# Two conditioned convolution layers on one core: order of the weight blocks, full-width weight products, and the small network in shifted steps

## The chip, the cores and the metric

The program runs on one core of one Trainium2 chip. The metric is the device time of one execution in microseconds (us), and the median of several runs is compared. The profile is of one execution of its own, so times read from its trace are those of that execution.

## The reference

Two layers are applied in turn to an activation `x` of 32 x 32 samples, 64 channels and 256 positions. In each layer the weights of a 3-tap convolution are made by a small network, for each of 32 x 256 places of its own. Cut to what matters:

```
def conv_ref(x, z, W1, b1, g1, be1, W2, b2, Wb1, bb1, gb1, beb1, Wb2, bb2):
    h = relu(ln(z @ W1 + b1, g1, be1))                 # z: (32, 256, 16) -> h: (32, 256, 128)
    w = (h @ W2 + b2).reshape(B, L, CI, CO, K)         # 128 -> 64 * 64 * 3 weights for each place
    hb = relu(ln(z @ Wb1 + bb1, gb1, beb1))
    bias = (hb @ Wb2 + bb2).transpose(0, 2, 1)         # (32, 64, 256)
    x_uf = stack([pad(x)[..., i:i + L] for i in range(K)], axis=-1)
    return einsum('sbilk,bliok->sbol', x_uf, w) + bias[None]

x = x + conv_ref(group_norm(x), ...layer 0...)
x = x + conv_ref(group_norm(x), ...layer 1...)
```

All is float32. The group norm has 32 groups over the last axis and takes its statistics over the whole of a sample's values in a group.

## The kernel before

**Rounds.** The work of a layer is cut into 32 units `u` (4 samples of the batch, 64 of the 256 positions each), and a unit into two halves `h` of the output channels. The main loop runs over `v`, 128 rounds for both layers. In round `v` the weights of half `v` are made (`weights`, 12 blocks) and the products of half `v - 1` are taken (`products`). The order within a round is written out by hand: `weights(v, 0)` makes its first block, then come the products of the round before (`between`), then the eviction of that block and the other 11 blocks, with the side work of `agenda(v)` behind them.

**Blocks.** A block is one tile `pg` (128 x 8 x 128, three buffers in PSUM) with the weights of 8 output channels of one *kind*. The convolution pairs even and odd positions, so a tile holds two of the three taps: the lower 64 partitions one tap, the upper 64 another. `make` takes two products for each of the 8 channels: 64 columns of `w2` against one half of the hidden tile `h` (its even or its odd positions). Kinds 0 and 1 use the same half of `h` for both, kind 2 uses even below and odd above. `take` adds the bias `b2` and writes into the one tile `wall`: kinds 0 and 1 with one VectorE addition over 128 partitions, kind 2 (its two halves go to different places) with a VectorE addition of the lower half and eight ScalarE activations of the upper. Each round goes through four groups of 8 channels, kinds 0, 1, 2 in each. `products` reads all of `wall` and `xn`, in 32-column products, and VectorE adds the result to `ring`, which holds residual and bias.

**The opening.** Before the rounds, `first_phase` walks through 22 steps `i`. Each takes statistics of four pieces of `x` on VectorE (`stats`) and reloads the piece's buffer, one of four. Among the steps stand the small network (`Batch`, 8 batches of four hidden tiles), and from step 6 on the 12 blocks of round 0 (`first_weights`). A batch has links in this order: `form` (TensorE), `variance` (VectorE, ScalarE), `scale` (VectorE, GpSimd), `turn` (TensorE transposes, a copy on ScalarE), `hidden` (TensorE, ScalarE, stores to `hd` in DRAM) and four times `bias` (TensorE, ScalarE, stores to `bd` in DRAM). Batch j begins in step 1 + 2j with form, variance and scale, turns in the next, has its hidden tiles in the one after and its four biases in the fourth. Step 18 (`needed`) has the statistics that the first norm needs; steps 18 and 19 merge them, lay the table and normalize the first tile (`starting`).

**Queues.** All loads go through SP's queue in program order, so a load that waits for its buffer holds those behind it. The stores of hidden tiles and biases are issued by ScalarE, between its own operations.

Of the kernel before, what the change touches and what calls it, by code (L numbers as in the profile page):

```python
# [23 lines left out]
FP = mybir.dt.float32  # L24
# [19 lines left out]
def conv_layers(  # L44
# [40 lines left out]
    hd = [dram.tile([P, 2 * 2 * M], FP, name=f"hd_{i}") for i in range(U // 2)]  # L85
    bd = [dram.tile([2, NT, C, LT], FP, name=f"bd_{i}") for i in range(U // 2)]
# [51 lines left out]
    def load_hidden(i):  # L138

        h = hp.tile([P, 2, 2, M], FP, tag="hT", name="hT")  # L140
        nc.sync.dma_start(out=h.rearrange("p b a m -> p (b a m)"), in_=hd[i])
        for b in range(2):
            hs[2 * i + b] = h[:, b]
# [78 lines left out]
    class Batch:  # L222


        def __init__(self, nets, zts, zps, zs, j):
            self.j, self.zt, self.zp, self.zs = j, zts[j % 2], zps[j % 2], zs
# [8 lines left out]

            self.q = take(BLK)
            self.zq = take(2 * BLK).rearrange("p (n f) -> p n f", n=2)
            self.ht = [[take(2 * BLK) for _ in range(2)] for _ in range(2)]
            self.bs = [take(BLK // 2).rearrange("p (t a m) -> p t a m", t=NT, a=2) for _ in range(2)]
            self.var = take(2 * NR * NR)  # L240
# [49 lines left out]
        def hidden(self, net):  # L290
# [8 lines left out]
            for k in range(2):  # L299
# [9 lines left out]
                for r in range(2):  # L309
                    nc.scalar.dma_start(  # L310
                        out=hd[self.j * NR + 2 * k + r], in_=self.ht[0][k][:, r * BLK : (r + 1) * BLK]
                    )

        def bias(self, i):
# [12 lines left out]
            bs = self.bs[i % 2]  # L327
# [115 lines left out]
    def first_phase(first_weights, first_bias, add_bias, starting):  # L443
# [22 lines left out]
        with tc.tile_pool(name="stage", bufs=1) as stage:  # L466
            zts, zps = [], []
            for j in range(2):
                zts.append(stage.tile([P, BLK], FP, name=f"zt_{j}"))
                zps.append(stage.tile([P, NR * NR * A], FP, name=f"zp_{j}"))  # L470
                nc.gpsimd.memset(zts[j], 1.0)
            zs = raw[:, 0 : 2 * BLK].rearrange("p (n r a) -> p n r a", n=2, a=R)

            def load_z(j):
                if j < U // 2 // NR:
                    n, i = divmod(j * NR, UL // 2)
                    for r in range(NR):
                        nc.sync.dma_start(
                            out=zts[j % 2][r * R : r * R + A],
                            in_=layers[n]["z"][:, (i + r) * BLK : (i + r + 1) * BLK],  # L480
                        )
                    w = NR * NR * A
                    nc.sync.dma_start(out=zps[j % 2], in_=layers[n]["zp"][:, i // NR * w : (i // NR + 1) * w])
# [5 lines left out]
            nets.append(Network(stage, layers[1], 1))  # L489
            nc.gpsimd.memset(zs, 0.0)  # L490
            load(2)
            load(3)
            load_z(1)
            for n in range(NL):
                load_b2(n)
            stats(0, range(LAND))
            nets[0].prepare(stage)
            count = U // 2 // NR
            made = {}
            begins = {1 + 2 * j: j for j in range(count)}  # L500

            def begun(i):
                j = begins.get(i)
                return None if j is None else made[j]

            for i in range(1, units):
                b = begun(i - 3)
                if b:
                    for k in range(NR):
                        b.bias(k)  # L510
                b = begun(i - 2)
                if b:
                    b.hidden(0)
                    b.hidden(1)
                b = begun(i - 1)
                if b:
                    b.turn()
# [416 lines left out]
```

## Time and profile before

| | |
|---|---|
| median of 3 runs | 4251.6 us (4250.24 to 4263.0) |
| profiled execution: its time | 4265.69 us |
| profiled execution: its span | 4263.9 us |
| TensorE products, weight loads, busy | 90%, 86% of the span |
| VectorE, ScalarE, GpSimd, busy | 61%, 30%, 45% |
| granted TensorE clock, mean | 0.986 |
| HBM read and written | 496.91 MB, 148.90 MB |

The page puts the time of an execution into its engines. A record of a float32 product is one of its two passes, records overlap, and a weight load runs beside the products. So a pace is read from the starts of records, and a wait from the time between the start of one and that of the next.

### The profile page before, as it was taken

How to read it: one execution, taken by the hardware profiler on the slowest of the kernel's cores; microseconds unless marked ns; L12 is line 12 of the kernel's file. 1: busy time of each engine (PE TensorE's matmuls, PEld its weight loads, DVE VectorE, ACT ScalarE, POOL GpSimd, SP SyncE). 2: the span in 40 equal slices, each digit the busy share in tenths (PEclk: the TensorE clock that was granted, in tenths of full speed). 3: DMA queues.
4: the chain of work that ended last, by engine and by line, in shares of the span. 5: the costliest groups of instructions: out<-in, count | busy, mean ns of one | idle time of the engine just before them, and what ended most of it. 6: DMA issues, size and time to landing. Idle time of an engine off the chain costs nothing.

```text
span 4263.9 us, 185545 instructions
## 1 busy us (share of the span) xinstructions
PE 3827.1 (90%) x86548; PEld 3683.7 (86%) x86548; DVE 2586.3 (61%) x2954; ACT 1288.1 (30%) x4431; POOL 1935.4 (45%) x655
## 2 busy tenths in 40 slices
PE   5669999999999999999998999999999999999998
PEld 3368898989989889899988999989889898898988
DVE  3366776777767776666665555555555555555555
ACT  2323233332333323323233222322323222232222
POOL 1034444444453444444454555545445544544551
PEclk9779999999999999999999999999999999999999
DMA  6565564655546555444478676777867777777772
GB/s 214 166 219 160 180 180 154 191 167 181 178 155 187 170 165 156 125 151 140 136 175 159 143 143 132 150 130 148 140 136 147 130 155 132 132 147 132 155 130 81
DMA packets 648724, 657.77 MB, mean 154 GB/s; under 512 B 563848, under 2 KB 572432, under 8 KB 582160
## 3 DMA queue, kind: packets, MB, share of 16 engines
q1 hardware_dynamic: 625936, 633.31, 61.7%
q8 instruction: 677, 11.09, 1.2%
q10 hardware_dynamic: 22016, 12.59, 1.0%
q14 instruction: 95, 0.78, 0.1%
HBM read 496.91 MB, written 148.90 MB: 151 GB/s over the span
## 4 chain that ended last, share of the span: by engine, by line
PE 74%; DMA 4%; ACT 4%; issue 4%; DVE 3%; POOL 2%; SPq 1%; ACTq 0%; POOLq 0%
PE pg L634 45%; PE pc L688 22%; PE pg L635 7%; DMA bt<-bd 4%; ACT wall L657 4%; DVE wall L646 3%; POOL ring L578 2%; SPq L571 1%; SPq L184 0%; DVE ring L697 0%; PE spread L419 0%; SPq L728 0%; SPq L583 0%; PE pe L598 0%; DVE first_parts L735 0%
## 5 line engine op out<-in xcount | busy, mean ns | idle before, releaser
L634 PE MATMUL pg<-hT,w2t 128*64 128x128 f32 x24576 | 2750.5, 274 | 28.9 <-issue 19.3
L635 PE MATMUL pg<-hT,w2t 128*64 128x128 f32 x24576 | 2752.7, 274 | 18.0 <-issue 17.6
L634 PEld LDWEIGHTS pg<-hT,w2t 128*64 128x64 f32 x24576 | 2687.2, 137 | 61.4 <-issue 39.3
L635 PEld LDWEIGHTS pg<-hT,w2t 128*64 128x64 f32 x24576 | 2686.9, 137 | 25.4 <-issue 24.8
L646 DVE TENSOR_TENSOR wall<-pg,b 128x1024 f32<-128x1024 f32 (+1 forms) x1536 | 1871.9, 1219 | 687.0 <-PE pg L635 681.2
L657 ACT ACTIVATE wall<-pg,b 64x128 f32<-64x128 f32 x4096 | 1158.2, 462 | 2191.5 <-DVE wall L646 2187.6
L688 PE MATMUL pc<-wall,xn 128*32 128x128 f32 (+1 forms) x36864 | 953.2, 263 | 282.1 <-ACT wall L657 137.4
L688 PEld LDWEIGHTS pc<-wall,xn 128*32 128x32 f32 x36864 | 917.9, 111 | 327.3 <-ACT wall L657 154.6
L578 POOL TENSOR_TENSOR ring<-ring,bt 128x2048 f32<-128x2048 f32 x127 | 577.6, 4548 | 1309.5 <-DMA bt<-bd 1030.8
L697 DVE TENSOR_TENSOR ring<-pc,ring 128x512 f32<-128x512 f32 x512 | 353.9, 691 | 843.3 <-PE pc L688 843.3
L620 POOL TENSOR_TENSOR xn<-raw,tab 128x2112 f32<-128x2112 f32 x86 | 438.9, 5104 | 568.0 <-PE pc L688 521.7
L620 POOL TENSOR_TENSOR xn<-xn,tab 128x2112 f32<-128x2112 f32 x126 | 591.8, 4697 | 9.9
L620 POOL TENSOR_TENSOR xn<-land,tab 128x2112 f32<-128x2112 f32 x40 | 224.7, 5617 | 106.4 <-DMA land<-x 106.2
L344 DVE BATCH_NORM_STATS2 parts<-ring 128x6 f32<-128x256 f32 x512 | 192.1, 417 | 6.5
L593 ACT COPY rim<-ring 128x64 f32<-128x64 f32 x64 | 19.5, 305 | 532.6 <-DVE ring L697 516.2
L735 DVE BATCH_NORM_STATS2 first_parts<-land 128x6 f32<-128x512 f32 x168 | 114.2, 680 | 3.0 <-DMA land<-in_xg_dram 2.9
L274 POOL TENSOR_TENSOR raw<-zp,xn 128x256 f32<-128x256 f32 x16 | 10.3, 644 | 173.5 <-DVE xn L269 82.9
L298 PE MATMUL ph<-xn,wc 17*128 17x512 f32 x128 | 41.3, 1061 | 39.1 <-ACT xn L288 37.7
L436 POOL COPY tab<-spot 64x1024 f32<-64x1024 f32 x28 | 29.0, 1035 | 86.7 <-ACT spot L423 85.8
L298 PEld LDWEIGHTS ph<-xn,wc 17*128 17x128 f32 x128 | 12.6, 295 | 58.2 <-ACT xn L288 39.7
L259 DVE TENSOR_TENSOR xn<-pt,zp 128x256 f32<-128x256 f32 x16 | 6.0, 419 | 74.6 <-PE pt L246 74.6
L461 DVE BATCH_NORM_STATS2 first_parts<-ring 128x6 f32<-128x512 f32 x72 | 44.5, 676 | 10.0 <-DMA ring<-in_xg_dram 9.9
(87 smaller groups left out, 390.2 us busy)
## 6 DMA issues: line engine op xcount, KB each, us to landing
bt<-bd SPq DMA_DIRECT2D x508, 256.0 KB, 10.8
ring<-in_xs_dram SPq DMA_DIRECT2D x64, 1024.0 KB, 11.7
x<-ring SPq DMA_DIRECT2D x64, 1024.0 KB, 4.9
ring<-x SPq DMA_DIRECT2D x64, 1024.0 KB, 9.6
out_dram<-ring SPq DMA_DIRECT2D x64, 1024.0 KB, 4.8
raw<-in_xp_dram SPq DMA_DIRECT2D x55, 1056.0 KB, 14.2
land<-in_xg_dram SPq DMA_DIRECT2D x46, 1024.0 KB, 7.8
raw<-x SPq DMA_DIRECT2D x128, 256.0 KB, 8.9
```

The lines of the kernel that those rows point to most:

```text
L298: nc.tensor.matmul(p[:, r], self.w.wc[x, net], self.zq[x, net], start=True, stop=True)
L344: nc.vector.bn_stats(out, y.rearrange("p o (a m) -> p o a m", a=2)[:, :, :, g * e : (g + 1) * e])
L461: nc.vector.bn_stats(first_parts[:, g, bg], slots[order[i]][:, k])
L578: nc.gpsimd.tensor_tensor(y, y, bts.pop(v), ALU.add)
L620: eng.tensor_tensor(o, i, tab[:, x, None, j0:j1].to_broadcast(list(o.shape)), op)
L634: nc.tensor.matmul(pg[0:C, k, :], w[:, k0 * C : (k0 + 1) * C], h0, start=True, stop=True)
L635: nc.tensor.matmul(pg[C:P, k, :], w[:, k1 * C : (k1 + 1) * C], h1, start=True, stop=True)
L646: nc.vector.tensor_tensor(place(rows, a), pg[rows].rearrange("p o (t m) -> p t m o", t=NT), b2[n][rows, kind, None, None, o0 : o0 + OG].to ...
L657: nc.scalar.activation(place(rows, a)[:, :, :, k], pg[rows, k].rearrange("p (t m) -> p t m", t=NT), AF.Identity, bias=b2[n][rows, kind, o0 ...
L688: nc.tensor.matmul(pc[t * S : (t + 1) * S, n0 - q * EB : n1 - q * EB, :], xn[:, u % 2, t, p, :], wall[:, t, a : a + (n1 - n0) * CH], start ...
L697: nc.vector.tensor_tensor(part, pc.rearrange("p (m a) o -> p o a m", a=2), part, ALU.add)
L735: nc.vector.bn_stats(first_parts[:, g, bg], lands[i % LAND])
```

## The change

Three things change.

1. *Order of the kinds.* A group's blocks are made in the order 0, 2, 1, so that a round ends with kind 1.
2. *Width of the product.* For kinds 0 and 1 one product with 128 columns of `w2` takes the place of two with 64. The 128 columns lie side by side: taps 1 and 2 for kind 0, taps 0 and 1 for kind 1. Kind 2 stays as it was.
3. *The small network.* All of a layer's `z` and `zp` is loaded at once, into the second half of `w2`, which is empty until step 17. All batches exist from the start. Batch j has `form` in step 2j, `variance` and `scale` in step 2j + 1, `turn` in step 2j + 2, `hidden` in step 2j + 3, and two biases each in steps 2j + 4 and 2j + 5. The biases have four buffers in place of two, and hidden tiles and biases are stored by one DMA each in place of two, for which `hd` and `bd` are laid out anew. The batch's buffers lie otherwise in `xn`; the first half of `w2` is loaded ahead of the steps instead of in step 2, the first hidden tiles in step 6 instead of 5, the first bias in step 18 instead of 16, and the blocks of round 0 stand in steps 7 to 18 instead of 6 to 17.

```diff
-    hd = [dram.tile([P, 2 * 2 * M], FP, name=f"hd_{i}") for i in range(U // 2)]
-    bd = [dram.tile([2, NT, C, LT], FP, name=f"bd_{i}") for i in range(U // 2)]
+    hd = [dram.tile([P, 2 * BLK], FP, name=f"hd_{i}") for i in range(U // 4)]
+    bd = [dram.tile([NT, 2, C, LT], FP, name=f"bd_{i}") for i in range(U // 2)]
...
-            self.q = take(BLK)
-            self.zq = take(2 * BLK).rearrange("p (n f) -> p n f", n=2)
-            self.ht = [[take(2 * BLK) for _ in range(2)] for _ in range(2)]
-            self.bs = [take(BLK // 2).rearrange(...) for _ in range(2)]
-            self.var = take(2 * NR * NR)
+            ht = [take(2 * BLK) for _ in range(2)]
+            self.bs = [take(BLK // 2).rearrange(...) for _ in range(4)]
+            self.var = take(2 * NR * NR)
+            o = flat.shape[1] // 2
+            self.ht = [[take(2 * BLK) for _ in range(2)], ht]
+            self.q = take(BLK)
+            self.zq = take(2 * BLK).rearrange("p (n f) -> p n f", n=2)
...
-                for r in range(2):
-                    nc.scalar.dma_start(
-                        out=hd[self.j * NR + 2 * k + r], in_=self.ht[0][k][:, r * BLK : (r + 1) * BLK]
-                    )
+                nc.scalar.dma_start(out=hd[self.j * NR // 2 + k], in_=self.ht[0][k])
...
-            for b in range(2):
-                nc.scalar.dma_start(
-                    out=bd[i][b].rearrange("t o l -> o t l"),
-                    in_=bs[b * C : (b + 1) * C].rearrange("p t a m -> p t (a m)"),
-                )
+            nc.scalar.dma_start(
+                out=bd[i].rearrange("t b o l -> (b o) t l"), in_=bs.rearrange("p t a m -> p t (a m)")
+            )
...
+            half_w2 = w2[:, CH:].rearrange("p o c -> p (o c)")
+            zts = half_w2[:, 0:w].rearrange("p (j f) -> p j f", j=count)
+            zps = half_w2[:, w : w + count * NR * NR * A].rearrange("p (j f) -> p j f", j=count)
+            def load_z(n):
+                js = slice(n * nl, (n + 1) * nl)
+                nc.gpsimd.memset(zts[:, js], 1.0)
+                z = layers[n]["z"].rearrange("a (j r f) -> r a j f", j=nl, r=NR)
+                for r in range(NR):
+                    nc.sync.dma_start(out=zts[r * R : r * R + A, js], in_=z[r])
+                nc.sync.dma_start(out=zps[:, js], in_=layers[n]["zp"].rearrange("p (j f) -> p j f", j=nl))
...
+            load_w2(0, 0, CH)
+            made = [Batch(nets, zts[:, j], zps[:, j], zs, j) for j in range(count)]
+            for i in range(units):
+                j, odd = divmod(i, 2)
+                if batch(j - 2):
+                    for k in range(2 * odd, 2 * odd + 2):
+                        batch(j - 2).bias(k)
+                if odd:
+                    if batch(j):
+                        batch(j).variance()
+                    if batch(j - 1):
+                        batch(j - 1).hidden(0)
+                        batch(j - 1).hidden(1)
+                else:
+                    if batch(j):
+                        batch(j).form()
+                    if batch(j - 1):
+                        batch(j - 1).turn()
...
+                if odd and batch(j):
+                    batch(j).scale()
...
+                if i == needed:
+                    first_bias()
...
-            (k0, h0), (k1, h1) = (((1, odd), (2, odd)), ((0, even), (1, even)), ((2, even), (0, odd)))[kind]
             for k in range(OG):
                 w = w2[:, o0 + k, :]
-                nc.tensor.matmul(pg[0:C, k, :], w[:, k0 * C : (k0 + 1) * C], h0, start=True, stop=True)
-                nc.tensor.matmul(pg[C:P, k, :], w[:, k1 * C : (k1 + 1) * C], h1, start=True, stop=True)
+                if kind < 2:
+                    cols = slice((1 - kind) * C, (3 - kind) * C)
+                    nc.tensor.matmul(pg[:, k, :], w[:, cols], (odd, even)[kind], start=True, stop=True)
+                else:
+                    nc.tensor.matmul(pg[0:C, k, :], w[:, 2 * C :], even, start=True, stop=True)
+                    nc.tensor.matmul(pg[C:P, k, :], w[:, 0:C], odd, start=True, stop=True)
...
-        order = [(kind, o) for o in starts for kind in (0, 1, 2)]
+        order = [(kind, o) for o in starts for kind in (0, 2, 1)]
...
-            if kind == 2 and u % UL == UL - 1 and n + 1 < NL:
+            if kind == 1 and u % UL == UL - 1 and n + 1 < NL:
                 load_w2(n + 1, o0, o0 + OG)
```

## Rows read from the trace of the kernel before

**Rows 1.** The page's costliest groups: busy us, mean ns, idle before and its releasers.

```profile
L634 PE MATMUL pg<-hT,w2t 128*64 128x128 f32 x24576 | 2750.5, 274 | 28.9 <-issue 19.3
L635 PE MATMUL pg<-hT,w2t 128*64 128x128 f32 x24576 | 2752.7, 274 | 18.0 <-issue 17.6
```

**Rows 2.** Timeline of TensorE, first passes of two rounds: start us, us, engine, line.

```profile
2033.35 0.32 PE L634 MATMUL pg<-hT,w2t 128*64 128x128 f32 x1
...
2063.58 0.32 PE L634 MATMUL pg<-hT,w2t 128*64 128x128 f32 x1
```

**Rows 3.** Timelines of VectorE, ScalarE and TensorE at the end of that round.

```profile
2051.08 1.23 DVE L646 TENSOR_TENSOR wall<-pg,b 128x1024 f32<-128x1024 f32 x1 [0.52 <-PE pg L635]
2052.83 1.22 DVE L646 TENSOR_TENSOR wall<-pg,b 64x1024 f32<-64x1024 f32 x1 [0.52 <-PE pg L635]
...
2054.14 2.25 ACT L657 ACTIVATE wall<-pg,b 64x128 f32<-64x128 f32 x8 [2.96 <-DVE wall L646]
...
2054.25 0.27 PE L634 MATMUL pg<-hT,w2t 128*64 128x128 f32 x1
...
2056.44 0.43 PE L688 MATMUL pc<-wall,xn 128*32 128x64 f32 x12 [1.91 <-ACT wall L657]
```

**Rows 4.** Waits of TensorE from 300 us on: us in total, times, longest.

```profile
PE pc L688 <- ACT wall L657: 135.6, 70, 3.7
PE pc L688 <- issue: 117.3, 86, 2.8
```

**Rows 5.** Timelines of VectorE, GpSimd and TensorE over the opening.

```profile
22.61 0.75 DVE L259 TENSOR_TENSOR xn<-pt,zp 128x256 f32<-128x256 f32 x2 [0.97 <-PE pt L246]
...
191.83 0.75 DVE L259 TENSOR_TENSOR xn<-pt,zp 128x256 f32<-128x256 f32 x2 [14.49 <-PE pt L246]
...
214.28 4.52 POOL L578 TENSOR_TENSOR ring<-ring,xn 128x2048 f32<-128x2048 f32 x1 [17.50 <-DMA xn<-bd]
...
250.04 0.43 PE L688 MATMUL pc<-wall,xn 128*32 128x64 f32 x4 [2.80 <-DVE xn L623]
```

**Rows 6.** Windows: us, busy us of PE, PEld, DVE, ACT, POOL (records), granted clock, DMA share, GB/s.

```profile
0.00:250.00 250.00, 137.72 (x824) 84.79 (x824) 89.56 (x175) 83.07 (x146) 27.18 (x48) 0.81 0.61 198
100.00:200.00 100.00, 67.71 (x470) 42.78 (x472) 38.47 (x65) 39.88 (x70) 6.14 (x17) 0.73 0.54 167
```

**Rows 7.** 128-column operations: timeline, one line's records with ns min/median/max, a window's clock.

```profile
1609.16 0.53 PEld L374 LDWEIGHTS over<-apart,same 128*128 128x128 f32 x4
...
L374 PEld LDWEIGHTS over<-apart,same x4: 192/192/193, 1609.2 to 1609.5; 128*128 128x128 f32 x4
...
92.96 2.18 PE L246 MATMUL pt<-form,zt 128*128 128x136 f32 x8 [1.03 <-ACT xn L300]
...
92.90:95.00 2.10, 2.04 (x8) 1.86 (x8) 0.00 (x0) 1.20 (x3) 0.00 (x0) 0.50 0.65 242
```

**Rows 8.** Timelines of TensorE's products and loads around one edge transpose (line 598).

```profile
2005.70 0.27 PE L634 MATMUL pg<-hT,w2t 128*64 128x128 f32 x1
...
2005.90 0.14 PEld L598 LDWEIGHTS pe<-ident,rim 128*128 128x128 f32 x1 [0.17 <-issue]
...
2006.17 0.32 PE L634 MATMUL pg<-hT,w2t 128*64 128x128 f32 x1
...
2006.33 0.27 PE L634 MATMUL pg<-hT,w2t 128*64 128x128 f32 x1
```

**Rows 9.** ScalarE in one batch of the opening (timeline), and its waits up to 250 us.

```profile
149.99 1.37 ACTq L335 DMA_DIRECT2D bd<-xn  x2
154.75 0.47 ACT L328 ACTIVATE xn<-pb,vec 128x256 f32<-128x256 f32 x1 [4.79 <-DMA bd<-xn]
...
160.00 1.20 ACT L300 ACTIVATE xn<-ph,vec 128x1024 f32<-128x1024 f32 x1 [2.18 <-PE ph L298]
161.23 0.82 ACTq L310 DMA_DIRECT2D hd<-xn  x2
...
ACT xn L328 <- DMA bd<-xn: 44.2, 10, 7.6
```

More of the change, by code (lines that the diff above doesn't have):

```diff
@@ L140, in load_hidden @@
         h = hp.tile([P, 2, 2, M], FP, tag="hT", name="hT")
-        nc.sync.dma_start(out=h.rearrange("p b a m -> p (b a m)"), in_=hd[i])
+        nc.sync.dma_start(out=h.rearrange("p b a m -> p (b a m)"), in_=hd[i // 2][:, i % 2 * BLK : (i % 2 + 1) * BLK])
         for b in range(2):
@@ L234, in take @@
                 return flat[:, o - n : o]
+            ht = [take(2 * BLK) for _ in range(2)]
+            self.bs = [take(BLK // 2).rearrange("p (t a m) -> p t a m", t=NT, a=2) for _ in range(4)]
+            self.var = take(2 * NR * NR)
+            o = flat.shape[1] // 2
+            self.ht = [[take(2 * BLK) for _ in range(2)], ht]
             self.q = take(BLK)
             self.zq = take(2 * BLK).rearrange("p (n f) -> p n f", n=2)
-            self.ht = [[take(2 * BLK) for _ in range(2)] for _ in range(2)]
-            self.bs = [take(BLK // 2).rearrange("p (t a m) -> p t a m", t=NT, a=2) for _ in range(2)]
-            self.var = take(2 * NR * NR)
         def form(self):
@@ L466, in first_phase @@
         with tc.tile_pool(name="stage", bufs=1) as stage:
[L467 to L483, printed above, removed]
+            count = U // 2 // NR
+            half_w2 = w2[:, CH:].rearrange("p o c -> p (o c)")
+            w = count * BLK
+            zts = half_w2[:, 0:w].rearrange("p (j f) -> p j f", j=count)
+            zps = half_w2[:, w : w + count * NR * NR * A].rearrange("p (j f) -> p j f", j=count)
+            nl = count // NL
+            def load_z(n):
[4 more added lines that the diff above has]
+                    nc.sync.dma_start(out=zts[r * R : r * R + A, js], in_=z[r])
+                nc.sync.dma_start(
+                    out=zps[:, js], in_=layers[n]["zp"].rearrange("p (j f) -> p j f", j=nl)
+                )
             nets = [Network(stage, layers[0], 0)]
@@ L495, in first_phase, with batch @@
                 load_b2(n)
-            stats(0, range(LAND))
             nets[0].prepare(stage)
[L498 to L517, printed above, removed]
-                if i in begins:
-                    made[begins[i]] = Batch(nets, zts, zps, zs, begins[i])
-                b = begun(i)
-                if b:
-                    b.form()
+            load_w2(0, 0, CH)
+            made = [Batch(nets, zts[:, j], zps[:, j], zs, j) for j in range(count)]
+            def batch(j):
+                return made[j] if 0 <= j < count else None
+            for i in range(units):
[14 more added lines that the diff above has]
+                        batch(j - 1).turn()
                 if i == needed:
@@ L533, in first_phase @@
                 stats(i, range(2))
-                if b:
-                    b.variance()
                 if i == needed:
@@ L538, in first_phase @@
                 stats(i, range(2, LAND))
-                if b:
-                    b.scale()
-                    load_z(b.j + 2)
-                if i == 2:
-                    load_w2(0, 0, CH)
+                if odd and batch(j):
+                    batch(j).scale()
                 if i == 3:
                     nets[1].prepare(stage)
-                if i == 5:
-                    for j in range(2):
-                        load_hidden(j)
-                if i == needed - 3:
+                if i == 6:
+                    for x in range(2):
+                        load_hidden(x)
+                if i == needed - 2:
                     load_half(0, 1, land)
-                if i == needed - 2:
                     load_residual(0)
-                    first_bias()
                 if i == needed - 1:
```

16 lines of the change are left out of this document (9 added, 7 removed).

## The prediction

> **What bounds the kernel now.** I read the page's costliest groups first. The weights products lead: 24576 records on line 634 and as many on 635, each line busy for some 2750 us of the span of 4263.9 [rows 1]. A product leaves two records on its line, one per pass of its float32 operands (128 rounds x 12 blocks x 8 products x 2 = 24576), and the two lines run side by side in the two halves of the array. So their means of 274 ns cannot be added up; the pace is read from a timeline.
>
> The timelines of one clean round (a value of v) give the sum of a round. Its first weights pass starts at 2033.35 and the next round's at 2063.58, so a round lasts 30.23 us [rows 2]. VectorE takes one finished block of weights every 1.75 us (2051.08 to 2052.83) [rows 3]; a block is 8 weights of 2 passes, 16 passes, so a pass (both halves together) costs 0.109 us. The round's last pass on line 634 starts at 2054.25, which is 20.90 us after the first. Then TensorE stands until 2056.44, 2.19 us, and the products run to the next round, 7.14 us [rows 2, 3]. 20.90 + 2.19 + 7.14 = 30.23.
>
> The wait of 2.19 us is the one that can be won. The reader is to see its chain: the last block is of the shared kind, VectorE adds its lower half at 2052.83 for 1.22 us, ScalarE adds the upper half only after that (2054.14, 2.25 us), and the products start 0.05 us later [rows 3]. Over the rounds the list of waits has 135.6 us of products behind that ScalarE line and 117.3 us named "issue" [rows 4]; the two sum to 252.9 us, which is 127 rounds at 1.99 us, so I read most of that "issue" as the same wait under another name. True fetch stalls show where no semaphore is in play: 19.3 + 17.6 = 36.9 us on lines 634 and 635 [rows 1].
>
> Then the opening. Its products start at 250.04 us [rows 5], and 127 rounds of 31.6 us on the mean follow ((4263.9 - 250) / 127). In those 250 us TensorE is busy 137.7 us at a mean granted clock of 0.81, and the DMA engines 61% [rows 6]: nothing is full, so the order of the work sets the pace. VectorE's first small-network product (line 259) comes at 22.61 and its eighth and last at 191.83: 7 batches in 169.2 us, 24.2 us each [rows 5].
>
> **The change part by part.** Times are against the profiled execution's 4265.7 us (span 4263.9); the median of the three runs is 4251.6, 14.1 us lower, and the forecast is given on that scale by taking the same difference off it.
>
> *Shared kind second.* Blocks come as 0, 2, 1, so the round ends on a kind that VectorE alone takes. ScalarE's part now belongs to the last block but one. From that block's last pass to the products takes 3.94 us by ScalarE's chain (2056.44 less 2052.50, which is 16 passes before 2054.25) [rows 3]. In that time TensorE has two blocks of 16 passes left, 32 x 0.111 = 3.55 us, and two mode switches of about 0.19 and 0.20 us (below): 3.94 us. The two chains meet, so the wait falls from 2.19 us to the switch's 0.20 us: **-1.99 us a round**. If ScalarE came 0.5 us later, 0.5 us of it would come back; the three tiles of `pg` do not bind, since the next user of the shared tile comes three blocks later, over 5 us.
>
> *One 128-column product.* For 8 of 12 blocks two half-width products become one full-width product. TensorE's streaming is not cut: two halves already run in one pass of 0.109 us, and the full-width pass streams the same 128 columns of activations. What is new is a weight load of 128 columns per pass instead of two parallel ones of 64. No row shows this very stream at the full clock, so I bound it. Below: a load that hides costs nothing, 0.109 us as now. Above: four 128-column float32 loads with tiny moving operands take 0.53 us, (0.53 - 0.19) / 3 = 0.113 us apart [rows 7], and if the load sets the pace a pass costs that. I take the middle, 0.111: 128 passes a round x 0.002 = **+0.26 us** (0 to +0.51).
>
> *The mode switches.* A round had two changes of column width (64 to 32 and back). With 128, 64, 128 in each of four triples it has seven more: four from 64 to 128, three from 128 to 64. The trace has the pair around the edge transpose, a lone 128-column operation between 64-column passes: pass at 2005.70, its load only at 2005.90, next 64-column pass at 2006.17, and the one after at 2006.33 [rows 8]. In the flow a pass follows after 0.109 us, so 0.09 us is idle before the load. The first load after a switch isn't hidden: the pass after 2006.17 comes 0.16 us later, 0.05 too late for 64 columns; I take 0.10 for 128. Into the wide mode: 0.09 + 0.10 = 0.19; out of it: 0.09 + 0.05, some 0.15. 4 x 0.19 + 3 x 0.15 = **+1.21 us a round** (0.9 if the wide load hides behind the idle time, 1.5 if each switch costs 0.2).
>
> The trace thus shows 0.09 us of standing per switch that no semaphore explains [rows 8]. The Trainium skill, "TensorEngine Tiling (Array Packing)", section Key Properties, says the same as a rule: a change of tiling mode, unlike a change of tile, drains TensorE. By that rule the seven switches each stand 0.09 us and the sum of this part is as above; were it not to hold between 64 and 128 in the steady flow, 7 x 0.09 = 0.63 us a round, 80 us in all, would stay away. The trace agrees with the rule.
>
> Sum of a round: -1.99 + 0.26 + 1.21 = -0.52 us; x 127 = **-66 us** (ends: -1.99 + 0 + 0.9 = -1.09, -138 us; -1.99 + 0.51 + 1.5 = +0.02, +3 us).
>
> *Fewer instructions.* A round's weights go from 768 TensorE instructions to 512. The fetch stalls among them, 36.9 us, fall by up to all of it; I take the same third: **-12 us** (0 to -37).
>
> *The opening.* ScalarE's rows of one batch show why a batch takes 24 us: bias evictions that each wait behind two DMA issues (1.37 us), 4.79 us of waiting for a bias buffer to be written out, and 2.18 us of waiting for the hidden product that needs the turned tile just copied [rows 9]. Over the opening the wait for the biases' writes is 44.2 us in 10 [rows 9]. The change gives the biases four buffers and one DMA issue in place of two, one issue in place of two for the hidden tiles, and sets the links of a batch in different steps (form, then variance, turn, hidden, two and two biases), so that neither wait stands in ScalarE's line. It also loads z once per layer into the unused half of `w2`, so that SP's queue no longer holds a ring load behind a z tile that is in use. What is left for ScalarE in a batch is 9.7 us of work (39.88 in 100 us [rows 6], x 24.2) and its issues, now 4 x 1.37 for biases and 2 x 0.82 for hidden tiles [rows 9], 7.1 us: 16.8, or 13.3 with the issues halved. TensorE has 67.71 us of work in 100 us, 16 us a batch, at a granted clock of 0.73 [rows 6]. So I take 18 us a batch: 7 x 6.2 = 43 us, and some 7 us for the last biases, whose wait stands ahead of the merge: **-50 us**. Ends: 0 if clock or DMA keep the pace, and -75 if the batches come at 15 us (7 x 9.2 = 64, and 11 at the end). The floor is 0.61 x 250 = 152 us of DMA work.
>
> Moved steps: w2's first half (3 MB) now stands on SP's queue ahead of the fifth ring load, and the first bias load comes two steps later, behind w2's second half. Before, the first bias add on GpSimd began at 214.28 after waiting 17.5 us for that load and ended 31 us ahead of the products [rows 5]; two steps of 9 to 12 us use most of that. If it is late, the products' first eviction on VectorE waits, and TensorE behind it: up to 5 us, once. The z fills on GpSimd and the moved 128-column products' VectorE adds change nothing in a round: VectorE has 0.5 us of idle time before each block [rows 3].
>
> Sum: -66 - 12 - 50 = -128 us; 4265.7 - 128 = 4137.7, and on the median's scale 4123.6, so **4124 us**.
>
> **The rivals.**
> 1. *The opening keeps its pace.* DMA at 61% and a clock of 0.73 speak for it, the waits inside ScalarE's line against it. Only the rounds change: -78 us, 4174.
> 2. *Switches or loads cheaper than I take them.* The round gains 1.09 us (-138) and the opening 50 or more, -188 or beyond: 4060. For it speaks that the load of 64 columns hides wholly in the flow, against it the 0.113 us between bare loads.
> 3. *The full-width pass is dearer; slower than before.* One mechanism: each pass of the 8 wide blocks waits for its load. The rest of the change is worth 128 us, 1.0 us a round, 8 ns a pass, so it decides at 0.119 us a pass; at 0.125 the loss is 0.014 x 128 x 127 = 228 us, less 128: +100, 4350. Against it stands 0.113 as the pace of loads alone; for it, that no row has load and float32 stream together at the full clock.
> 4. *The wide load is not hidden at all.* Then a pass is 0.109 + 0.109: 0.107 x 128 x 127 = +1740 us over my sum, about 5860. Against it: at a granted clock of 0.50, the 1.2 GHz level, eight 128-column loads and their passes of 136 columns take 2.18 us, 0.27 us each with the first load and the last drain in it. Streaming alone takes 2 x 0.109 x 136 / 128 = 0.23 there; with an unhidden load it would be 0.23 + 2 x 0.113 = 0.46 [rows 7]. The Trainium skill, "TensorE: Matmul & The Clock Gate", Part 3 under The mechanism's list of what overlaps, has it that weight loads overlap running products only where the row group differs, and here it is the same. By that rule this rival would hold; the trace disagrees.
> 5. *ScalarE still ends last.* The change then does only part of what it says; 0.5 us late costs 64 us: 4187.
>
> **How the numbers follow.** A measurement of this kernel can tell about 0.3% (13 us) from no change. Forecast 0.52; rival 1 0.13; rival 5 0.08; rival 2 0.12: all faster, 0.85. Rival 3 0.09 and rival 4 0.02: of rival 3's, 0.05 lies near its point of decision, no change; so slower 0.06 there and in rival 4, and 0.04 is left for mishaps of the opening that I cannot name. Faster 0.85, same 0.05, slower 0.10. The range takes in rivals 1, 2 and 5 and leaves out 3 and 4: 4055 to 4205.
>
> **What would show it.** Products should start about 0.2 us after the round's last weights pass, with the wait for line 657 gone or small. Wide passes should follow each other at 0.109 to 0.113 us, blocks of two wide kinds at 1.78, with gaps of about 0.3 us where the width changes. A clean round should last 29.7 us. The first products should start near 200 us, batches 18 us apart, with no wait of ScalarE for bias writes. The prediction is wrong if wide passes come 0.12 us apart or more, if the opening still ends near 250, or if a width change costs much more or nothing.

## The result and the profile after

The changed kernel takes 4078.0 us (median of 4 runs, 4077.01 to 4079.56) against 4250.92 of the kernel before: a ratio of 0.9587, interval 0.957 to 0.9605. That is 4.1% faster, 46 us below the forecast of 4124 and inside the range. The profiled execution took 4077.95 us with a span of 4076.2, 187.7 us less than the span of before; that span is of an execution 14 us above the median of its kernel, and the medians lie 172.9 us apart.

The weights products are now on three lines. These are the costliest groups of the page (busy us, mean ns, idle before and its releasers); line 622 is the full-width product, lines 624 and 625 the two halves of the shared kind:

```profile
L622 PE MATMUL pg<-hT,w2t 128*128 128x128 f32 x16384 | 1975.2, 279 | 1.3 <-ACT wall L647 0.7
L622 PEld LDWEIGHTS pg<-hT,w2t 128*128 128x128 f32 x16384 | 1877.1, 192 | 94.3 <-issue 85.5
L624 PE MATMUL pg<-hT,w2t 128*64 128x128 f32 x8192 | 1007.5, 276 | 3.5 <-issue 2.3
L625 PE MATMUL pg<-hT,w2t 128*64 128x128 f32 x8192 | 1008.0, 276 | 0.0
```

Against [rows 1], the idle time ahead of weights products has nearly gone, 1.3 + 3.5 us where it was 28.9 + 18.0. A full-width load is busy 192 ns, and yet it doesn't hold the stream up, as the second of the next two views shows.

One clean round of the changed kernel, first as its lines' extents (records, ns min/median/max, first and last start), then as TensorE's timeline at the end of that round:

```profile
L678 PE MATMUL pc<-wall,xn x288: 219/272/273, 1978.9 to 1985.9; 128*32 128x128 f32 x112, 128*32 128x64 f32 x32
L624 PE MATMUL pg<-hT,w2t x64: 272/273/324, 1986.0 to 2004.7; 128*64 128x128 f32 x64
L622 PE MATMUL pg<-hT,w2t x128: 275/275/377, 1987.9 to 2008.5; 128*128 128x128 f32 x128
```

```profile
2007.59 1.17 PE L622 MATMUL pg<-hT,w2t 128*128 128x128 f32 x9
2008.68 0.26 PE L678 MATMUL pc<-wall,xn 128*32 128x64 f32 x4
```

From products to products the round lasts 2008.68 - 1978.88 = 29.8 us, where it was 30.23 [rows 2]. Its weights run from 1986.0 to 2008.5, 22.5 us where they took 20.90, and the products follow the last pass after 0.2 us, where it was 2.19 [rows 3]. Nine wide passes in 1.17 us, the last of them 0.275 long (the line of L622 above has 275 ns), are (1.17 - 0.275) / 8 = 0.112 us apart.

TensorE's products at a change from 128 to 64 columns, and products and loads at a change from 64 to 128 (timelines):

```profile
1987.92 3.84 PE L622 MATMUL pg<-hT,w2t 128*128 128x128 f32 x32
1991.69 0.32 PE L624 MATMUL pg<-hT,w2t 128*64 128x128 f32 x1
1991.85 0.27 PE L624 MATMUL pg<-hT,w2t 128*64 128x128 f32 x1
1991.96 0.27 PE L624 MATMUL pg<-hT,w2t 128*64 128x128 f32 x1
...
2017.52 0.27 PE L624 MATMUL pg<-hT,w2t 128*64 128x128 f32 x1
...
2017.72 0.86 PEld L622 LDWEIGHTS pg<-hT,w2t 128*128 128x128 f32 x7 [0.17 <-issue]
2017.73 0.94 PE L622 MATMUL pg<-hT,w2t 128*128 128x128 f32 x6
```

Into the wide mode: 2017.73 is 0.21 us after the last narrow pass, 0.10 more than in the flow, and the six passes of 0.94 us leave 0.94 - 0.275 - 4 x 0.112 = 0.22 us for the first of the five distances, 0.10 more than in the flow again: 0.20 us. Out of it: the last of the 32 wide passes starts 0.275 us before the group's end, at 1991.49, the next pass at 1991.69, 0.09 us late, and the one behind it after 0.16, 0.05 late: 0.14 us. All changes from 330 us on are alike: 485 into the wide mode, with first distances of 0.208 to 0.210 us for nine in ten, and 332 out of it, with 0.205.

VectorE, ScalarE and TensorE at the end of another round (timelines), against [rows 3]:

```profile
2035.92 1.22 DVE L636 TENSOR_TENSOR wall<-pg,b 64x1024 f32<-64x1024 f32 x1 [0.68 <-PE pg L625]
2037.24 2.26 ACT L647 ACTIVATE wall<-pg,b 64x128 f32<-64x128 f32 x8 [3.40 <-DVE wall L636]
2037.90 1.22 DVE L636 TENSOR_TENSOR wall<-pg,b 128x1024 f32<-128x1024 f32 x1 [0.75 <-PE pg L622]
2039.59 0.43 PE L678 MATMUL pc<-wall,xn 128*32 128x64 f32 x12
```

VectorE's last block now follows the shared one, and ScalarE ends at 2039.50, 0.09 us before the products. The two chains meet, as the prediction worked out, and there is no slack between them: in the kernel before, where every round waits for ScalarE, the products start 0.05 to 0.10 us after its end. The gap tells the two apart. In half of the rounds it is 0.205 us, as in grouped_wide below, where ScalarE ends some 5 us earlier; in most of the others ScalarE ends 0.10 us ahead and the gap is 0.22 to 0.23, so ScalarE still holds those rounds by some 0.02 us.

TensorE's waits from 300 us on (us in total, times, longest):

```profile
PE pe L586 <- ACT rim L581: 20.6, 31, 0.8
PE pc L678 <- issue: 11.1, 27, 1.5
PE pg L624 <- issue: 2.3, 4, 1.6
PE pc L678 <- ACT wall L647: 1.7, 1, 1.7
```

The 252.9 us of [rows 4] are 12.8 now. At the top stands a wait that the prediction didn't have: the edge transposes of line 586 wait for the copy of the rim. ScalarE and TensorE at one of them (timelines):

```profile
2019.68 2.26 ACT L647 ACTIVATE wall<-pg,b 64x128 f32<-64x128 f32 x8 [11.08 <-DVE wall L636]
2021.96 0.30 ACT L581 COPY rim<-ring 128x64 f32<-128x64 f32 x1
...
2022.32 0.33 PE L586 MATMUL pe<-ident,rim 128*128 128x128 f32 x1 [0.75 <-ACT rim L581]
```

With the shared block second, its eight activations come ahead of the rim copy (of the edges that the transpose turns) on ScalarE, and TensorE stands 0.75 us at the transpose.

The opening of the changed kernel (timelines; last the third round's first products), and those first products in the kernel before:

```profile
17.61 0.76 DVE L261 TENSOR_TENSOR xn<-pt,w2t 128x256 f32<-128x256 f32 x2
132.62 0.74 DVE L261 TENSOR_TENSOR xn<-pt,w2t 128x256 f32<-128x256 f32 x2
180.19 4.49 POOL L566 TENSOR_TENSOR ring<-ring,xn 128x2048 f32<-128x2048 f32 x1 [40.31 <-DMA xn<-bd]
180.44 4.86 DVE L608 TENSOR_TENSOR xn<-land,tab 128x576 f32<-128x576 f32 x1
180.56 0.31 PE L678 MATMUL pc<-wall,xn 128*32 128x64 f32 x4 [1.96 <-DVE xn L611]
185.33 0.76 DVE L608 TENSOR_TENSOR xn<-xn,tab 128x576 f32<-128x576 f32 x1
186.33 6.34 PE L678 MATMUL pc<-wall,xn 128*32 128x64 f32 x140 [5.46 <-DVE xn L611]
261.85 1.41 PE L678 MATMUL pc<-wall,xn 128*32 128x64 f32 x48
```

```profile
328.43 0.83 PE L688 MATMUL pc<-wall,xn 128*32 128x64 f32 x24 [2.48 <-issue]
```

The first products start at 180.56 where they started at 250.04 [rows 5], 69.5 us earlier, and 66.6 us of that last until the third round. The eight batches run from 17.61 to 132.62, 16.4 us each, where they took 24.2. The windows of the page's columns, first the stretch ahead of the products, then one to set against [rows 6]:

```profile
0.00:180.00 180.00, 120.80 (x680) 79.18 (x680) 88.61 (x174) 81.90 (x146) 25.11 (x47) 0.82 0.82 272
100.00:200.00 100.00, 66.99 (x536) 47.05 (x537) 62.70 (x100) 43.41 (x87) 11.56 (x14) 0.75 0.70 232
```

Ahead of the products the DMA engines are now busy 0.82 of the time, 148 us in all, where the same 180 us of the kernel before have 0.61. The granted clock hardly moved, 0.75 in the second stretch after 0.73.

Between the third round's products and the last round's there are 125 rounds. The table is worked out from the starts of TensorE's records in them, us per round on the mean: products (first product to the first weights pass), weights (the distances between weights passes), gap (last weights pass to products), other (stretches around other products among them, the edge transposes above all), and the weights pauses, distances of over 0.26 us between two weights passes, as a sum over all rounds of what they are above the flow's 0.11 us, with their count. The last rows are kernels of the experiments below.

| kernel | products | weights | gap | other | round | weights pauses |
|---|---|---|---|---|---|---|
| before | 7.51 | 21.36 | 2.22 | 0.28 | 31.37 | 49.2 us, 61 |
| after | 7.37 | 22.39 | 0.23 | 0.43 | 30.41 | 2.2 us, 2 |
| order_only | 7.52 | 21.27 | 0.44 | 0.52 | 29.76 | 38.2 us, 51 |
| wide_only | 7.39 | 22.59 | 2.01 | 0.19 | 32.18 | 0.4 us, 1 |
| opening_only | 7.48 | 21.24 | 2.23 | 0.28 | 31.23 | 35.3 us, 55 |
| narrow | 7.46 | 21.26 | 0.45 | 0.51 | 29.69 | 35.9 us, 52 |
| edges_early | 7.35 | 22.40 | 0.23 | 0.21 | 30.19 | 2.6 us, 3 |
| narrow_edges | 7.50 | 21.37 | 0.44 | 0.28 | 29.59 | 49.5 us, 63 |
| shared_first | 7.54 | 21.41 | 0.21 | 0.33 | 29.50 | 52.7 us, 109 |

The rounds give 125 x 0.96 = 120 us and the opening 67, together 187 of the 187.7. The rounds of opening_only run the same instructions as those of before and are 0.14 us shorter, mostly by fewer pauses: two executions of the same rounds can differ by that much.

### The profile page after: what moved, and what is told of

The parts are those of the page before. It is cut to its first block, busy times and chain, and to the rows that moved or that the text cites. A ratio compares the mean times of both kernels' runs of the same rounds, so it can differ in the third digit from the quotient of the medians.

```text
span 4076.2 us, 152594 instructions
## 1 busy us (share of the span) xinstructions
PE 3960.9 (97%) x70164; PEld 3738.3 (92%) x70164; DVE 2599.5 (64%) x2954; ACT 1284.5 (32%) x4431; POOL 1935.3 (47%) x655
## 4 chain that ended last, share of the span: by engine, by line
PE 90%; DVE 3%; ACT 2%; issue 1%; ACTq 0%; DVEq 0%
PE pg L622 44%; PE pc L678 23%; PE pg L624 21%; ACT wall L647 2%; DVE wall L636 2%; PE pg L625 1%; DVE ring L687 1%; DVE parts L341 1%; DVE xn L608 0%; PE pe L586 0%; ACT rim L581 0%; PE over L371 0%; DVE first_parts L458 0%; PE spread L416 0%; ACT spot L420 0%
## 5 line engine op out<-in xcount | busy, mean ns | idle before, releaser
L622 PE MATMUL pg<-hT,w2t 128*128 128x128 f32 x16384 | 1975.2, 279 | 1.3 <-ACT wall L647 0.7
L622 PEld LDWEIGHTS pg<-hT,w2t 128*128 128x128 f32 x16384 | 1877.1, 192 | 94.3 <-issue 85.5
L624 PE MATMUL pg<-hT,w2t 128*64 128x128 f32 x8192 | 1007.5, 276 | 3.5 <-issue 2.3
L625 PE MATMUL pg<-hT,w2t 128*64 128x128 f32 x8192 | 1008.0, 276 | 0.0
L624 PEld LDWEIGHTS pg<-hT,w2t 128*64 128x64 f32 x8192 | 883.0, 137 | 62.3 <-issue 2.9
L625 PEld LDWEIGHTS pg<-hT,w2t 128*64 128x64 f32 x8192 | 882.8, 137 | 0.7 <-issue 0.6
L276 POOL TENSOR_TENSOR raw<-w2t,xn 128x256 f32<-128x256 f32 x16 | 10.3, 644 | 114.1 <-DVE xn L271 114.1
L458 DVE BATCH_NORM_STATS2 first_parts<-ring 128x6 f32<-128x512 f32 x72 | 44.2, 676 | 17.7 <-DMA ring<-in_xg_dram 17.7
```

The source lines that it names most:

```text
L622: nc.tensor.matmul(pg[:, k, :], w[:, cols], (odd, even)[kind], start=True, stop=True)
L624: nc.tensor.matmul(pg[0:C, k, :], w[:, 2 * C :], even, start=True, stop=True)
L625: nc.tensor.matmul(pg[C:P, k, :], w[:, 0:C], odd, start=True, stop=True)
```

## The experiments

The theory was that three parts work side by side: the order takes 2 us a round, the full-width product costs 1.5 us of it less the pauses that go with half of its instructions, and the opening gives 65 to 70 us. The rivals were that the full-width product helps, or that order and width need each other.

**order_only**: the kernel before, with the order of the kinds alone.

```diff
-        order = [(kind, o) for o in starts for kind in (0, 1, 2)]
+        order = [(kind, o) for o in starts for kind in (0, 2, 1)]
...
-            if kind == 2 and u % UL == UL - 1 and n + 1 < NL:
+            if kind == 1 and u % UL == UL - 1 and n + 1 < NL:
```

> The kernel before with the order 0, 2, 1 alone; products stay two of 64 columns, the opening stays. My theory: the wait after a round's last weights pass falls from 2.19 us to about 0.45 (ScalarE's chain of 3.94 us less 32 passes of 0.109), so a clean round lasts 28.5 us, and 127 x 1.74 = 221 us go; the edge transposes of the first layer now wait for ScalarE's eight activations, 0.7 us in 32 rounds, +20; the long pauses among the weights passes stay as they were, since the instructions do. 4050. Rival (the pauses among the weights come from the order, not from the number of instructions): they go as well, some 65 us more, 3985.

Measured: 4055.37 us beside 4253.49, ratio 0.9529 (0.9511 to 0.9546). The order (the second pair of lines only shifts the loads of the next layer's `w2`) is worth 198 us, more than the whole change. TensorE's waits from 300 us on:

```profile
PE pc L688 <- issue: 31.7, 89, 2.7
PE pe L598 <- ACT rim L593: 29.2, 32, 1.0
PE pg L634 <- issue: 18.4, 24, 2.1
PE pc L688 <- ACT wall L657: 12.2, 59, 1.9
PE pg L635 <- issue: 11.4, 16, 2.0
```

The gap is 0.44 us, not 0.2: without the width switches TensorE gets through its last two blocks faster, and ScalarE ends just behind it (12.2 us in 59 waits). The rim wait is here too, so it belongs to the order and not to the width.

**wide_only**: the kernel before, with the full-width product alone.

```diff
-                nc.tensor.matmul(pg[0:C, k, :], w[:, k0 * C : (k0 + 1) * C], h0, start=True, stop=True)
-                nc.tensor.matmul(pg[C:P, k, :], w[:, k1 * C : (k1 + 1) * C], h1, start=True, stop=True)
+                if kind < 2:
+                    cols = slice((1 - kind) * C, (3 - kind) * C)
+                    nc.tensor.matmul(pg[:, k, :], w[:, cols], (odd, even)[kind], start=True, stop=True)
+                else:
+                    ...
```

> The kernel before with the full-width product for kinds 0 and 1 alone; order 0, 1, 2, opening as before. My theory: 0.0025 us a pass for 128 passes, and seven switches on the path at 0.20 in and 0.15 out (the eighth hides in the wait for ScalarE): +1.4 us a round, +180; the pauses among the weights passes go with the instructions, -65: 4365. Rival (the pauses don't depend on the instructions): 4430. Rival (full width is what made the change fast): below 4251.

Measured: 4360.61 us, ratio 1.0247 (1.023 to 1.0264), so 107 us slower. The waits of its weights products from 300 us on, and its instruction queue (packets, MB, share; the row of the kernel before stands second):

```profile
PE pg L634 <- issue: 0.2, 1, 0.2
q8 instruction: 549, 8.99, 0.9%
```

```profile
q8 instruction: 677, 11.09, 1.2%
```

The 36.9 us of "issue" on lines 634 and 635 [rows 1] are gone to 0.2, with 128 packets fewer on the instruction queue, and the products pause less too (7.39 us where it was 7.51). That pays back a part only: the weights of a round without pauses and other work grow from 20.91 to 22.65 us, 1.74, and the mean round's still by 1.23.

**opening_only**: the changed kernel with the old order and the two 64-column products, so the new opening alone.

```diff
-                if kind < 2:
-                    ...
+                nc.tensor.matmul(pg[0:C, k, :], w[:, k0 * C : (k0 + 1) * C], h0, start=True, stop=True)
+                nc.tensor.matmul(pg[C:P, k, :], w[:, k1 * C : (k1 + 1) * C], h1, start=True, stop=True)
...
-        order = [(kind, o) for o in starts for kind in (0, 2, 1)]
+        order = [(kind, o) for o in starts for kind in (0, 1, 2)]
```

> The kernel after with order 0, 1, 2 and two 64-column products, so that only the small network's steps, buffers and DMAs are new. My theory: the first product starts near 180 us instead of 250 and the rounds are those of before: -67, 4184. Rival (the earlier start is given back in the first rounds, whose loads are not earlier): -40 or less, 4210.

Measured: 4189.19 us, ratio 0.9848 (0.9834 to 0.9863): 64 us, and by the traces it is the opening's: the products start at 180.9 where they started at 250.04.

**narrow**: the changed kernel with the two 64-column products, so order and opening without the width (the first part of the diff above).

> The kernel after with two 64-column products again: order and opening as changed, full width undone. My theory: the wide product costs 1.5 us a round in switches and loads and saves the fetch pauses of some 65 us and a wait of 0.25 us a round, so without it 127 x 1.3 = 165 us go and 65 come back: 3980. Rival (the pauses are gone for another reason than the instructions): 3915. Rival (the wide product is worth having): above 4078.

Measured: 3987.92 us, ratio 0.9374 (0.936 to 0.9388). It beats both kernels. Against the changed kernel the full-width product costs 90 us: in the table 22.39 - 21.26 = 1.13 us of weights a round, of which 0.22 come back in the gap, 0.09 in the products and 0.08 in the rest; 0.73 x 125 = 91.

**edges_early** and **narrow_edges**: the changed kernel, and narrow, with the rim copy one place earlier in the round, ahead of the shared block's activations on ScalarE; the transposes stay where they are.

```diff
-                todo[1].append(lambda: take_edges(v - 1))
+                todo[0].append(lambda: take_edges(v - 1))
```

> The kernel after with one line moved: the edge copy (take_edges) is issued to ScalarE before the eight activations of the round's second block instead of after them. My theory: the 32 edge transposes of the first layer wait for that copy because the shared block has moved ahead of it, 0.7 us each beyond their switches; without it 26 us of gaps between weights passes and other operations become 5: 4057. Rival (the transposes are late for another reason): 4078.

> The same line moved in the kernel with two 64-column products. My theory: 35 us of such gaps become 5: 3988 - 30 = 3958. Rival: 3988.

Measured: edges_early 4047.77 us, ratio 0.9513 (0.9499 to 0.9527); narrow_edges 3968.81 us, ratio 0.9318 (0.9303 to 0.9334). The wait for the rim is on neither list of waits any more, and the kernels gained 30 and 19 us. Of narrow_edges the column "other" fell by 0.23 us a round, 29 us, but this execution has 13.6 us more of weights pauses than that of narrow. In narrow_edges ScalarE still ends last in a clean round:

```profile
2106.77 2.26 ACT L645 ACTIVATE wall<-pg,b 64x128 f32<-64x128 f32 x8 [4.66 <-DVE wall L634]
2108.68 0.27 PE L622 MATMUL pg<-hT,w2t 128*64 128x128 f32 x1
2109.12 0.54 PE L676 MATMUL pc<-wall,xn 128*32 128x64 f32 x16 [0.16 <-issue]
```

ScalarE ends at 2109.03 and the products start 0.09 us later, 0.44 us behind the last weights pass, which is why "issue" there is again that wait by another name.

**grouped_wide** and **grouped_narrow**: edges_early and narrow_edges with all four blocks of a kind in a row. In the first this leaves two of the seven switches between 64 and 128 columns in a round.

```diff
-        order = [(kind, o) for o in starts for kind in (0, 2, 1)]
+        order = [(kind, o) for kind in (0, 2, 1) for o in starts]
```

> The kernel after with the edge copy early and the blocks of a round in the order 0 0 0 0 2 2 2 2 1 1 1 1, so that the width changes twice among the weights instead of seven times. My theory: five switches less (three in at 0.20, two out at 0.15) are 0.9 us a round, 110 us, and the edge copy 21: 3947. Rival (four shared blocks in a row pile up on ScalarE, 2.26 us each against 1.75 us of TensorE, and TensorE waits for a free tile 0.5 us or more a round): 4010 or above.

> The kernel with two 64-column products, the edge copy early and the grouped order. My theory: the wait ahead of the products falls from 0.46 to 0.2 us, 32 us in all, and the edge copy saves 30: 3926. Rival (pile-up on ScalarE as for the other grouped kernel): 3990 or above. Rival (the fetch pauses, which only the wide product removes, outweigh its two switches): the grouped wide kernel is the faster one.

Measured: grouped_wide 4032.62 us, ratio 0.9477 (0.9463 to 0.9491); grouped_narrow 4003.84 us, ratio 0.9411 (0.9397 to 0.9425). The theory fell by some 80 us in each, and the pile-up on ScalarE took its place. ScalarE and VectorE in one round of grouped_narrow (timelines), then a wait of TensorE's weight loads in it from 330 to 3900 us:

```profile
2012.48 8.41 ACT L645 ACTIVATE wall<-pg,b 64x128 f32<-64x128 f32 x32 [7.34 <-DVE wall L634]
...
2014.66 1.22 DVE L634 TENSOR_TENSOR wall<-pg,b 64x1024 f32<-64x1024 f32 x1 [0.53 <-PE pg L623]
2016.81 1.22 DVE L634 TENSOR_TENSOR wall<-pg,b 64x1024 f32<-64x1024 f32 x1 [0.93 <-PE pg L623]
2018.85 1.23 DVE L634 TENSOR_TENSOR wall<-pg,b 128x1024 f32<-128x1024 f32 x1 [0.83 <-PE pg L623]
```

```profile
PEld pg L622 <- ACT wall L645: 118.5, 341, 0.4
```

Four shared blocks in a row put 32 activations behind each other on ScalarE, 8.41 us, 2.1 us a block, where TensorE makes a block in 1.75 us. With three tiles TensorE then waits for a tile, and the blocks come 2.04 to 2.15 us apart. In the order 0, 2, 1 the two kinds of VectorE between them hide ScalarE. In grouped_wide such waits, at the start of three blocks in 118 rounds, come to 88 us by the starts of the passes. Of the 110 us that five switches less were to give, that leaves 22; it is 15 us faster than edges_early (4047.77 to 4032.62).

**shared_first**: narrow_edges with the shared kind first of each three, so that two of VectorE's own blocks end a round.

```diff
-        order = [(kind, o) for o in starts for kind in (0, 2, 1)]
+        order = [(kind, o) for o in starts for kind in (2, 0, 1)]
```

> This is narrow_edges (two 64-column products, the edge transposes in their earlier place) with the shared kind first of each group of three: shared, first, second. Theory: the length of the gap before the products depends on how many blocks that VectorE takes alone stand last in the round, so with two of them last instead of one the gap falls from 0.456 us to about 0.205 us, which is what the full-width kernel shows, and the time falls by 0.25 x 127 = 32 us from 3968.8 to about 3937 us, ratio 0.925. Rival: ScalarE takes its eight activations of the fourth group one block earlier or not is of no weight, the gap is the end of the last VectorE block itself and stays at 0.456 us, so the time stays at 3969 us, ratio 0.932. Second rival: the shared block now stands right behind the products, its eight activations delay ScalarE's work for the round's start (the rim copy), and the time rises to 3990 us or more.

Measured: 3959.49 us beside 4249.14, ratio 0.9315 (0.9299 to 0.9332). The gap fell as expected, from 0.44 to 0.21 us, and the shortest round from 28.50 to 28.26. But the 32 us did not come: by the ratio it is the time of narrow_edges (0.9318), and the 9 us between the two medians are not clear of noise. By the table 0.04 us a round went back into the products, 0.04 into the weights and 0.05 into the rest. Of the 109 pauses among the weights passes 54 stand at one place, ahead of the third block after the products, in rounds of the first layer, and there TensorE waits for VectorE. Such a wait of its weight loads from 300 us on, which narrow_edges does not have:

```profile
PEld pg L622 <- DVE wall L634: 16.4, 52, 0.3
```

Those 54 take 13 us, by the starts of the passes. So, as the second rival had it, a shared block right behind the products brings a wait at the start of the round, though for VectorE and not for the rim copy. The other 55 pauses, 39.7 us, compare with the 49.5 of narrow_edges. The two are the fastest kernels of this study, by the ratios both 2.8% below the changed one.

## Why the prediction was right, and where it was off

The sign and the range held, and most of the working: the sum was -128 us, the profiled executions show -188 and the medians -173.

*The gap.* Predicted -1.99 us a round, measured -2.00 (2.22 to 0.23). Rival 5, that ScalarE ends last all the same, holds for this kernel by some 0.02 us in about 50 of the 125 rounds and is out as a cost; without the width switches it holds in part (0.44 us in order_only).

*The full-width pass.* Predicted 0.111 us, measured 0.112. Rivals 3 and 4 are out: loads of 192 ns and products of the same rows go by at one in 0.112 us. The rule that rival 4 would follow from, in the list of what overlaps in the Trainium skill's "TensorE: Matmul & The Clock Gate", Part 3, The mechanism, lets a load overlap products only with another row group; that does not fit this stream. The paragraph ahead of that list also lets a load into a background weight buffer go ahead of products, which would.

*The switches.* Predicted 0.19 in and 0.15 out, measured 0.20 and 0.14. Rival 2 is out: the seven switches each stand about 0.09 to 0.10 us ahead of the first pass in the steady flow too. The Trainium skill, "TensorEngine Tiling (Array Packing)", Key Properties, has as a rule that a change of tiling mode drains TensorE; these rows agree. With 128 x 0.0025 = 0.32 us for the wide passes and 4 x 0.20 + 3 x 0.14 = 1.22 for the switches, the weights of a clean round should have grown by 1.54 us; they grew by 1.56.

*Fewer instructions: the term that was mis-sized.* The step was "I take the same third: -12 us (0 to -37)", from the 36.9 us of "issue" on the two weights lines. Nearly all of the weights' pauses went, not a third: 49.2 us in 61 pauses became 2.2 in 2, and wide_only shows that the width alone does it. The products lost 7.51 - 7.37 = 0.14 us a round besides, 17 us, which the prediction had no term for, because it read the "issue" of the products' line mostly as the wait for ScalarE. Of them 14 are pauses too: distances of over 0.2 us between two products come to 35.6 us in 58 before and to 21.6 in 43 after. So some 61 us of pauses came back where 12 was taken. Set against opening_only, whose rounds are those of the kernel before, it is 39 us (35.3 among the weights, 27.6 among the products): the size depends on the execution, and is above the 37 of the upper end in both. A clean round's weights grew by 22.46 - 20.90 = 1.56 us, 195 us over 125 rounds, the mean round's by only 1.03, 128 us; of the 67 us between them 47 are these pauses, and the cause of the other 20 stays open. What the pauses are, the last section shows.

*The opening.* Predicted -50 us with batches of 18 us; it gave 69.5 at the first products and 66.6 from the third round on. Batches came 16.4 us apart (7 x 7.74 = 54), the first began 5.0 us earlier (17.61 for 22.61), which had no term, and from the last batch to the products it took 47.9 us in place of 58.2, 10 for the 7 taken. Rival 1 is out. ScalarE waits for no bias write any more, and a bias's store is one issue of 0.37 us as a rule. The late first bias was foreseen: GpSimd's add waited 40.31 us for it and ran after the merge. TensorE stands 5.46 us ahead of the second group of products, near the 5 us of the prediction, but the way is another (below). What gave the shorter batches was not split: ScalarE's waits for bias writes, 44.2 us [rows 9], went, but so did most of another one. The loads of `x` (line 454) stood 64.7 us behind the small network's line 269 on SP's queue in the first 250 us of the kernel before, and 18.5 us in the changed one. The DMA engines now have 148 us of work in the 180 us ahead of the products, close to the 152 us that the prediction named as the floor, so some 30 us at most are left there.

*What was missed.* The rim wait, 20.6 us in 31. The prediction moved ScalarE's eight activations and asked only what they do to the round's end, not what stands behind them at the round's start.

*What the whole says.* The parts alone give -198, +107 and -64 us, -155 together where all three gave -173. Order and opening together give -265 in narrow, about their sum; the 18 us between lie in the width, which costs 107 us alone and 90 beside them. Alone it has an eighth switch, at the round's end (22.65 us of weights in a clean round for 22.46), and the 0.21 us that come back in the gap only pay for that one; beside the order 0.22 come back with seven. That would be 27 us a run, and no run separates it. The prediction had the order and the width right as terms, but summed them to -66 and left it there: the reader could have seen from its own -253 and +187 that the full-width product is a loss that the order pays for.

## What to carry to other kernels

When a change joins several edits, price each alone before adding them: here an order of blocks wins 198 us and a product that needs half the instructions loses 90, because the array was already full with two halves side by side and each change of width costs 0.14 to 0.20 us. Put work that needs two engines in a row early enough before a join that another block hides it, but not several such blocks behind each other, and look at what its second engine had to do next. "Issue" on a line can be a semaphore's wait and pauses of the instruction stream at once; count the pauses from the starts of records before giving either a price.

## What the hardware did that was not expected

*A VectorE addition stood still beside GpSimd's.* In the opening's rows VectorE's operation of 180.44 takes 4.86 us, with both inputs in SBUF, where its like takes 0.76; GpSimd's add had begun 0.25 us before and ended at 184.68. The same goes for all eight runs with the new opening: one operation of VectorE's line 608, whichever came first after the start of the add, took 4.55 to 4.94 us (in edges_early 2.66 after 2.71 of standing) and ended 0.54 to 0.62 us after the add, and the others of its shape 0.62 to 0.76. In before, order_only and wide_only the add ran 30 us or more earlier, and VectorE's four operations of 576 columns took 0.76 each. Rows of two of the eight (timelines), grouped_narrow first:

```profile
179.15 4.73 POOL L566 TENSOR_TENSOR ring<-ring,xn 128x2048 f32<-128x2048 f32 x1 [39.41 <-DMA xn<-bd]
179.94 4.55 DVE L608 TENSOR_TENSOR xn<-xn,tab 128x576 f32<-128x576 f32 x1 [0.41 <-ACT tab L433]
```

```profile
178.40 4.53 POOL L566 TENSOR_TENSOR ring<-ring,xn 128x2048 f32<-128x2048 f32 x1 [40.37 <-DMA xn<-bd]
178.66 4.82 DVE L608 TENSOR_TENSOR xn<-raw,tab 128x512 f32<-128x512 f32 x1
```

The Trainium skill, "SBUF — State Buffer", section SBUF: two separate sides, has the rule: VectorE with two inputs in SBUF and GpSimd take one shared pair of ports as a lock, and the later one waits for the whole of the other's instruction. These rows agree with it. The main loop's evictions read a tile in PSUM: 759 of the changed kernel's 1536 start while an addition of GpSimd's runs, and the longest takes 1.23 us.

*TensorE's instructions arrive late.* The pauses between weights passes that no semaphore explains fell from 49.2 us to 0.4 with a third fewer instructions among the weights (wide_only). The instruction queue's 11.09 MB came in 677 packets of 16 KB, 64 bytes for each of TensorE's 173096 records. In the kernel before 60 of the 61 pauses among the weights end 1.2 to 2.0 us after the end of such a packet, where 12% of all weights passes stand, and 57 of the 58 among the products, where 14% stand. In order_only, narrow and narrow_edges it is all 166 of the weights pauses. So TensorE stood there for its next instructions.
